# Spectrum, image and result moved in whole-partition transfers, the last product's rows in the spectrum's buffer, and a new order of steps

## The chip, the cores and the metric

The kernel runs on one core of one Trainium2 chip. The metric is the time of one execution on the device in microseconds (us). Its engines are TensorE (PE, matrix products; PEld is its weight load), VectorE (DVE), ScalarE (ACT), GpSimd (POOL) and SyncE (SP), which issues nearly all DMA transfers here.

## The reference

Input is x, 64 images of 96 channels and 56 x 56 pixels, f32. Three blocks follow one another, each on the whole image:

- A convolution block: a 1 x 1 product to 192 channels with a folded batch norm and silu; groups of channels shifted by one pixel and shuffled; a depthwise 3 x 3 convolution plus an identity branch, silu; a gate from the channels' means (two small grouped products, sigmoid); a 1 x 1 product back to 96 channels, plus x, silu.
- A spectral block over the 3136 pixels as one sequence: layer norm and a product to 192 channels with relu, a Fourier transform along the pixels, a complex diagonal product with biases and relu on each frequency, the inverse transform, a product back to 96 channels, added to its input.
- A feed-forward block with a layer norm in front, whose operands are rounded to 8-bit floats (5 exponent bits) and whose sums are rounded to 16 bits.

The Fourier transform of length 3136 is made as 56 x 56: a transform over one index (`f1`), twiddle factors and a transform over the other index (`f2`); only 29 of 56 rows of frequencies are kept, since the input is real. Between `f1` and `f2` the data must change from "rows on partitions" to "columns on partitions". That is done by storing to DRAM and loading back; the same is done on the way back, between `i1` and `i2`.

## The kernel before

One image is cut into steps, each a small function. `x_in` loads; `ea`, `eb` (first product), `eb_sh` (shift by DMA), `dw` (depthwise taps on PE), `gt` and `lt` (depthwise taps on DVE, 9 steps each), `se1`, `se2` (gate), `pj` (product back). Then `c`, `sp` (norm statistics), `w1`, `f1`, `f1_st` (store of the spectrum), `f2_ld` (its load), `f2`, `w2` (product), `i1`, `i1_st`, `i2_ld`, `i2`. Then `n`, `x`, `h`, `o` (norm, transposes, feed-forward) and `o_st`. A suffix tells the engine's part: `_mm` is PE, `_ev`, `_u`, `_r`, `_sq` are mostly ACT evacuations, `f2_s`, `f2_p`, `w1_ev`, `i2_ev`, `h_b`, `n_v`, `pj_add` are DVE.

The order of everything is written out by hand: `PLAN` gives each step of an image a time, image b adds b x 105, and all steps of all 64 images are issued in the order of these sums, under a manual schedule. Only the order counts; each engine then runs its list in order and waits where it must. Four images are in work at once, so `f2` of one image stands beside `dw` of the next one and `h` of the one before. `h_mm[6]` is the step h_mm with index 6.

Buffers that the steps share:

- `buf_h` holds, one after the other, `h_v` (output of `w1`), `pq_a` and `pq_b` (output of `f2_p`, read by `w2_mm`), and `p_v` (rows loaded by `i2_ld`, read by `i2_mm`).
- `buf_g` holds `g_v` (spectrum loaded by `f2_ld`, read by `f2_mm`), then `u_v` (output of `w2_ev`, read by `i1_mm`) and `q_v` (output of `i1_ev`, stored by `i1_st`).
- `psa`, two PSUM buffers in turn, takes the results of `w1`, `f1`, `f2`, `w2`, `i1` and `i2`; `psb`, four buffers, those of all other products.

The spectrum is loaded in four chunks of 8 (the last 5) frequency rows. Before each but the first, a tiny DMA that reads the chunk before (`probe`) keeps SP from issuing the next one until that one has landed. `f2_mm[0]` needs chunk 0, `f2_mm[2]` and `[1]` chunk 1, `f2_mm[3]` chunk 2, `f2_mm[4]` and `[5]` chunk 3:

```python
LD = ((0, 8), (8, 16), (16, 24), (24, NK))
def f2_ld(b, i):
    k0, k1 = LD[i]
    if i:
        nc.sync.dma_start(out=probe[0:1, 0:1], in_=g_v[64:65, LD[i - 1][0], 0:1])
    for r in range(2):
        nc.sync.dma_start(
            out=g_v[r * 64 : r * 64 + HW, k0:k1, :], in_=held["spec", b][:, r * 32 + k0 : r * 32 + k1, :]
        )
```

The 96 channels stand on partitions 0 to 47 and 64 to 111 of 112, so image and result are moved in two halves; partition 48 of the image holds ones inside the frame (it carries the first product's bias).

Of the kernel before, what the change touches and what calls it, by code (L numbers as in the profile page):

```python
# [7 lines left out]
F32 = mybir.dt.float32  # L8
# [7 lines left out]
C = 96  # L16
HW = 56
NPIX = HW * HW
MID = 192
HID = 384  # L20
CP = 112
TILES = ((0, 64), (64, CP))
GAP = 48
TP = 64
RPC = 8
NCH = HW // RPC
# [20 lines left out]
    "x_in": (-47.0873800, -43.2480721, -33.8184146, -42.4321669, -41.6983245, -49.6354125, -45.2970245),  # L47
    "ea_mm": (25.6687554, -18.6019459, -18.2766274, 16.8947317, 9.0890490, -20.9491366, 26.5234594),
    "ea_ev": (26.5961203, -12.8346944, -12.0558905, 18.3539585, 11.9892739, -18.0927155, 26.8208273),
    "eb_mm": (-24.2217280, -27.1252465, -28.5212136, -26.0439145),  # L50
    "eb_ev": (-24.1705572, -24.8159248, -27.0548028, -24.4210050),
    "eb_sh": (-7.7763780, -5.1891020, -14.3493101, -8.0736385),
    "eb_z": (-0.0568513,),
    "dw_mm": (27.1905859, 28.2270849, 30.0157383),
    "dw_ev": (32.6265507, 32.5419044, 34.0136867, 32.0626837),
    "gt": (
        18.5417590, 27.3932657, 28.4348554, 30.0405776, 30.3534777, 31.2679969, 32.1252342, 33.5617949, 35.3971287,
    ),
    "gs": (37.3295953,),
    "lt": (-3.4369246, 1.4154043, 8.9015990, 12.7386339, 14.9242937, 16.9569681, 19.0058087, 25.8181102, 27.2536815),  # L60
    "ls": (30.9696760,),
    "se1_mm": (38.1174920,),
    "se1_ev": (39.4012005,),
    "se2_mm": (39.9568261,),
    "se2_ev": (41.0093676,),
    "se2_th": (41.6370568,),
    "se2_pw": (42.7356286,),
    "pj_mm": (47.6293895, 48.0460084, 55.6924205, 56.2257124),
    "pj_add": (51.9548047, 52.9757229, 48.9486048, 52.4199992, 56.5208084, 56.3342891, 57.7357223, 58.9053497),
    "pj_ev": (52.4266468, 54.5563910, 49.5686264, 53.9975302, 57.3353294, 58.0358601, 64.2278724, 60.1034130),  # L70
    "c_mm": (68.6422640, 72.8958869, 66.4186663, 70.5016788, 73.7968378, 81.1540053, 75.3642593),
    "c_st": (69.1048996, 74.0834508, 69.6641726, 71.8469708, 79.6401411, 81.2770733, 76.3014887),
    "c_v": (77.3368996, 84.7421070),
    "c_pow": (80.4785931, 85.6468413),
    "sp_v": (83.0231830, 86.9442643),
    "sp_mm": (83.5958606, 91.6622997),
    "sp_ev": (84.6935666, 98.3470105),
    "sp_st": (84.9182307, 104.3262665),
    "w1_mm": (91.1847046, 99.3743923, 107.0630638, 109.7535225, 115.0779331, 117.7791802, 128.3897698),
    "w1_ev": (95.1158413, 101.3844416, 109.5428488, 112.4130173, 118.6707781, 121.0948441, 130.1859056),  # L80
    "f1_mm": (103.1645366, 103.6378920, 112.1950558, 112.9967147, 121.9973686, 123.2339179, 131.7418102),
    "f1_ev": (103.8752244, 106.2876092, 115.0341529, 116.5416927, 123.1240239, 126.3577447, 132.9203119),
    "f1_st": (105.0265754, 116.1773780, 117.6886644, 118.9203869, 126.8918215, 126.9985321, 135.1083565),
    "f2_ld": (135.1419010, 135.4933209, 140.1563600, 153.2148099),
    "f2_mm": (135.3144599, 144.2623043, 142.7071223, 149.0540458, 153.9987769, 158.4518856),
    "f2_u": (
        137.6614180, 139.5999755, 145.8963285, 148.6480681, 143.6745056, 144.3798314, 151.9081888, 154.2916813,
        154.8766840, 155.4088772, 160.1561499, 160.2407000,
    ),
    "f2_s": (  # L90
        140.6001249, 141.6781807, 148.1048425, 149.2120807, 145.7714192, 145.9139389, 152.5732992, 154.5515294,
        156.3172941, 156.6391862, 160.5955754, 160.7678822,
    ),
    "f2_r": (143.2110272, 151.0363931, 149.4970293, 156.5551535, 160.8170295, 165.3808270),
    "f2_p": (145.3432078, 151.4176571, 149.5496523, 158.2621001, 161.1258051, 167.6494558),
    "w2_mm": (159.7753575, 155.3022495, 161.7965796, 168.1185810),
    "w2_ev": (161.2536676, 157.1569605, 163.6822311, 171.1138835),
    "i1_mm": (162.6590790, 166.7961018, 174.2991711),
    "i1_ev": (166.3472470, 165.9292538, 169.1177355, 169.1485805, 176.9253459, 176.6408078),
    "i1_st": (174.9466660, 180.3925690, 182.4974982),  # L100
    "i2_ld": (188.6796396, 198.8294222),
    "i2_mm": (192.8792346, 192.2221249, 201.7637940, 200.8210782),
    "i2_ev": (197.2438881, 196.4091824, 193.4196408, 195.1684356, 205.0085736, 204.5692890, 201.3823970, 201.8192486),
    "n_mm": (199.2735303, 219.3462979, 198.1616011, 209.7155720, 217.1048197, 206.4557874, 216.1525940),
    "n_sq": (200.3838494, 223.0303187, 198.7625009, 212.4039709, 219.3987946, 208.1995030, 218.5954397),
    "n_v": (200.8599777, 223.0993290, 200.2251649, 217.3989652, 220.1840919, 209.9338724, 219.1855594),
    "n_pow": (201.5854245, 224.4817921, 203.3394463, 218.3771210, 221.4663650, 210.8600116, 220.4581247),
    "n_x": (204.8989415, 227.0802149, 207.1755708, 219.2080326, 226.6324331, 212.4013872, 223.1334093),
    "x_mm": (205.9313777, 228.0541936, 214.7407205, 222.1417630, 227.6089704, 214.9482177, 224.9828165),
    "x_ev": (215.5949267, 230.5744237, 217.0784037, 224.8320339, 228.9853364, 216.6319969, 227.3901209),  # L110
    "h_mm": (
        232.6842970, 233.0509672, 234.5689910, 233.8905234, 243.9705701, 231.1824963, 242.0876641, 249.3422780,
        247.6714562, 262.3158746, 249.5121590, 269.1269742, 245.6772976, 281.8579222, 275.5176718, 291.0115353,
        298.8948961, 298.6901683, 272.9130353, 274.8890827, 267.7027131,
    ),
    "h_ev": (
        233.2951821, 233.9892274, 235.1790311, 235.3740739, 245.7427623, 232.8851785, 246.7755713, 250.3102318,
        248.5727503, 264.8834302, 250.8738180, 272.1122460, 247.3449184, 285.4922975, 280.0758001, 292.5182940,
        298.9075518, 299.1057623, 275.2554216, 280.8510059, 271.9477751,
    ),  # L120
    "h_b": (
        233.3310183, 238.5879932, 239.6985884, 236.4106010, 248.1860080, 237.7565907, 247.4859421, 252.4799898,
        253.3286109, 265.1753247, 274.5160827, 273.6196081, 259.8167793, 289.1079857, 281.7059923, 295.2166748,
        313.0427147, 307.8153028, 280.3205727, 295.0172563, 303.2860349,
    ),
    "h_q": (
        235.1365714, 240.0903826, 240.2123523, 238.6786534, 249.8236945, 239.5739109, 249.1205248, 258.5058367,
        256.0111952, 266.4473323, 276.4671451, 279.2778238, 261.0771312, 290.1247931, 282.3662819, 298.7249474,
        314.1209334, 326.2464381, 296.9278791, 328.6751318, 314.9292593,
    ),  # L130
    "o_mm": (243.3019756, 251.4566128, 260.0349491, 292.9513206, 292.0855692, 335.3427890, 334.7225136),
    "o_ev": (252.4449030, 252.4462979, 260.7877533, 295.5347424, 297.3701267, 339.4824442, 335.9297802),
    "o_b": (253.4669270, 274.1077430, 267.6272919, 297.7581544, 311.6604822, 343.9355403, 344.9555045),
    "o_f": (256.7737436, 286.0913549, 285.2670749, 323.3039842, 337.3903643, 352.8603345, 353.4120892),
    "o_st": (258.9714075, 288.2940604, 307.3848207, 328.4555594, 347.7179313, 355.7939648, 378.3559833),
# [4 lines left out]
def conv_attn_ffn(  # L140
# [30 lines left out]
    tab_ones: bass.AP,  # L171
# [20 lines left out]
    nc.vector.memset(xi, 0.0)  # L192

    def load_x(b, i):

        rows = slice(i * RPC, (i + 1) * RPC)
        for p0, c0 in ((0, 0), (64, 48)):
            nc.sync.dma_start(  # L198
                out=xi[p0 : p0 + 48, 1 + i * RPC : 1 + (i + 1) * RPC, 1 : HW + 1],
                in_=x[b, c0 : c0 + 48, :].rearrange("c (a b) -> c a b", b=HW)[:, rows, :],  # L200
            )


    def load(ap, shape, name, eng=nc.sync, dtype=F32):
        t = const.tile(shape, dtype, name=name)
        eng.dma_start(out=t, in_=ap)
        return t

    ex_w = load(expand_t, [CP, MID], "ex_w")

    nc.sync.dma_start(out=xi[GAP : GAP + 1].rearrange("p a b -> p (a b)"), in_=tab_ones)
    for i in range(NCH):
        load_x(0, i)
    eps = const.tile([128, 1], F32, name="eps")
    nc.vector.memset(eps, 1e-5)
    mhalf = const.tile([128, NJ], F32, name="mhalf")
# [966 lines left out]
```

## Time and profile before

| | |
|---|---|
| median of 3 runs | 6605.18 us (6599.12 to 6605.9) |
| profiled execution, its own time | 6600.45 us |
| its span in the profile | 6598.6 us |
| mean granted TensorE clock | 0.973 |
| DMA packets | 976826, of them 641745 under 512 bytes; 740.73 MB |

Busy time of PE by step, from the groups by line between 2320 and 4317 us (20 images), divided by 20 and by the number of such steps in an image, in us: `ea_mm` 0.85, `eb_mm` 0.80, `dw_mm` 3.28 (three), `se1_mm` 0.54, `se2_mm` 0.78, `pj_mm` 1.8, 3.8, 2.1, 1.2, `c_mm` 0.50, `sp_mm` 0.26, `w1_mm` 1.52, `f1_mm` 0.81, `f2_mm` 2.03 (1.89, 1.65 and 1.27 for [1], [4] and [5]), `w2_mm` 2.4 (the last 1.6), `i1_mm` 1.75, `i2_mm` 1.28, `n_mm` 0.81, `x_mm` 0.34, `h_mm` 0.30, `o_mm` 0.69. They add up to 98.8 us an image, more than the PE busy time, because neighbouring lines overlap in the records. For DVE and ACT the mean of one instruction is taken: `lt` 1.86, `gt` 1.51, `w1_ev` 0.95, `f2_s` 1.30 and `f2_p` 1.10 (two instructions each), `i2_ev` 0.62, `n_v` 0.72, `h_b` 0.37, `pj_add` 0.57; `f2_u` 0.69, `f2_r` 0.9, `h_ev` 0.56, `h_q` 0.58, `pj_ev` 0.63, `w2_ev` 0.79, `o_b` 0.68, `dw_ev` 0.87, `gs` 1.44. These overlap by some 10%, too.

How to read the profile: the page's line of busy time gives an engine's busy time, its share of the span and its number of instructions. In the windows view a row is a stretch, its length, the busy time and number of instructions of PE, PEld, DVE, ACT and POOL, then the granted clock, the DMA engines' share and GB/s. In the waits view "A <- B: t, n, m" says that A's engine sat idle for B, t us in all, n times, m the longest. In the chain of waits each row is a start, a length and what ran; SPq is SP issuing. L numbers are lines of the kernel before.

### The profile page before, as it was taken

The page shows a single profiled execution, that of the slowest core. Times are in us where ns is not written, and L with a number is a line of the kernel's source. Part 1 is how long each engine was busy: PE and PEld are TensorE (multiplying, and loading weights), DVE is VectorE, ACT ScalarE, POOL GpSimd, SP SyncE. Part 2 cuts the span into 40 slices and gives each one's busy share as a digit, 9 for nine tenths or more (in the row PEclk, how much of TensorE's full clock was granted, in tenths as well). Part 3 has the DMA queues.
Part 4 walks back from the last instruction along what each step waited for, and adds up shares of the span by engine and source line. Part 5 has one row for each costly group of instructions (what it writes and reads, how often), then busy time and mean ns, then how long its engine had stood idle before and what let it go on. Part 6 is the DMA issues. An engine that isn't in the chain of part 4 may idle for free.

```text
span 6598.6 us, 217772 instructions
## 1 busy us (share of the span) xinstructions
PE 5970.6 (90%) x92162; PEld 4023.3 (61%) x92162; DVE 5271.5 (80%) x9939; ACT 4990.7 (76%) x10830; POOL 1660.2 (25%) x1100
## 2 busy tenths in 40 slices
PE   4999999999999999999999999999999999999986
PEld 2666666666666666666666666666666666666664
DVE  6788787787887887887877878878878878778773
ACT  2677777777777777777777777777777777777776
POOL 1122222222222222222222222222222222222222
PEclk8999999999999999999999999999999999999997
DMA  3444444444444444444444444444444444444442
GB/s 83 105 113 119 112 110 120 117 107 118 114 116 116 116 114 115 112 116 113 110 121 117 107 118 114 116 116 111 118 111 109 123 112 111 120 118 106 121 103 74
DMA packets 976826, 740.73 MB, mean 112 GB/s; under 512 B 641745, under 2 KB 916889, under 8 KB 975721
## 3 DMA queue, kind: packets, MB, share of 16 engines
q1 hardware_dynamic: 973130, 725.03, 44.4%
q8 instruction: 725, 11.88, 0.8%
q10 hardware_dynamic: 2720, 1.77, 0.1%
q14 instruction: 251, 2.06, 0.1%
HBM read 329.68 MB, written 341.31 MB: 102 GB/s over the span
## 4 chain that ended last, share of the span: by engine, by line
DVE 30%; DMA 21%; ACT 21%; PE 13%; SPq 6%; issue 6%; POOL 3%; DVEq 0%; POOLq 0%; ACTq 0%
DMA buf_g<-spec 10%; DVE d_last L508 7%; DMA buf_h<-rows 6%; DVE ue L799 4%; DVE s L796 4%; ACT y L954 4%; ACT ue L780 3%; PE ps_eb L421 3%; DMA spec<-fs 3%; POOL rs L922 3%; PE psa L755 3%; ACT h L965 2%; DVE buf_h L809 2%; SPq L198 2%; DVE buf_h L692 2%
## 5 line engine op out<-in xcount | busy, mean ns | idle before, releaser
L987 POOL TENSOR_TENSOR o<-t,o 112x448 f32<-112x448 f32 x448 | 684.2, 1528 | 3322.6 <-ACT o L981 2100.4
L508 DVE SCALAR_TENSOR_TENSOR d_last<-e_b,taps,d_last 128x1568 f32<-128x1568 f32 x512 | 954.3, 1864 | 0.5
L965 ACT CAST h<-y 128x448 fp8e5<-128x448 f16 x1344 | 756.2, 582 | 236.8 <-DVE y L959 224.5
L922 POOL TENSOR_TENSOR rs<-v,mhalf 128x4 f32<-128x4 f32 x448 | 609.8, 1374 | 926.4 <-DVE v L623 669.9
L954 ACT CAST y<-ps_h 128x448 f16<-128x448 f32 x1344 | 679.4, 556 | 161.2 <-PE ps_h L949 158.1
L495 DVE SCALAR_TENSOR_TENSOR d_vec<-e_a,taps,d_vec 128x1120 f32<-128x1120 f32 x512 | 770.8, 1505 | 11.6
L687 PE MATMUL psa<-w1c,t 112*128 112x192 f32 x3584 | 684.9, 334 | 9.9 <-DVE t L906 9.7
L755 PE MATMUL psa<-l_tab,buf_g 128*64 128x112 f32 x7424 | 477.1, 287 | 233.0 <-DMA buf_g<-spec 191.6
L755 PEld LDWEIGHTS psa<-l_tab,buf_g 128*64 128x64 f32 x7424 | 419.9, 153 | 409.4 <-issue 271.8
L474 PE MATMUL ps_d<-e_a,diag 32*32 32x504 f32 x18432 | 629.4, 590 | 0.0
L929 ACT ACTIVATE xt<-ps_n,rs 128x96 fp8e5<-128x96 f32 x1792 | 465.4, 377 | 198.6 <-POOL rs L922 190.1
L687 PEld LDWEIGHTS psa<-w1c,t 112*128 112x128 f32 x3584 | 579.8, 190 | 50.8 <-DVE t L906 17.5
L959 DVE TENSOR_SCALAR y<-y,qb 128x448 f16<-128x448 f16 x1344 | 472.1, 371 | 112.7 <-ACT y L954 103.5
L809 DVE SCALAR_TENSOR_TENSOR buf_h<-ue,s 128x448 f32<-128x448 f32 (+2 forms) x768 | 423.7, 600 | 159.6 <-ACT s L803 157.9
L637 DVE BATCH_NORM_STATS2 st<-ps_c 128x6 f32<-128x96 f32 x1792 | 326.2, 251 | 278.7 <-PE ps_c L629 272.4
L474 PEld LDWEIGHTS ps_d<-e_a,diag 32*32 32x32 f32 x18432 | 395.7, 103 | 214.9 <-ACT e_a L411 37.9
L780 ACT ACTIVATE ue<-psa,fa 128x448 f32<-128x448 f32 (+1 forms) x512 | 346.5, 690 | 229.6 <-PE psa L755 124.7
L692 DVE SCALAR_TENSOR_TENSOR buf_h<-psa,rs 128x768 f32<-128x768 f32 x448 | 426.8, 953 | 69.6 <-PE psa L687 69.6
L656 POOL TENSOR_TENSOR rs<-v,mhalf 128x16 f32<-128x16 f32 (+1 forms) x128 | 333.6, 2606 | 582.8 <-DVE v L651 582.8
L949 PE MATMUL ps_h<-xq,q 96*128 96x448 fp8e5 x1344 | 409.1, 360 | 72.3 <-ACT y L954 45.3
L796 DVE SCALAR_TENSOR_TENSOR s<-psa,fa,ue 128x448 f32<-128x448 f32 (+1 forms) x512 | 325.5, 636 | 181.3 <-ACT ue L780 180.8
L906 DVE SCALAR_TENSOR_TENSOR t<-psa,bn2c_b,t 112x392 f32<-112x392 f32 x512 | 291.7, 621 | 155.2 <-PE psa L894 151.9
(172 smaller groups left out, 11948.6 us busy)
## 6 DMA issues: line engine op xcount, KB each, us to landing
spec<-fs SPq DMA_DIRECT2D x896, 192.0 KB
buf_g<-spec SPq DMA_DIRECT2D x384, 336.0 KB
buf_h<-rows SPq DMA_DIRECT2D x128, 672.0 KB
x<-in_x SPq DMA_DIRECT2D x896, 84.0 KB
out_dram<-o SPq DMA_DIRECT2D x896, 84.0 KB
rows<-buf_g SPq DMA_DIRECT2D x128, 420.0 KB
rows<-buf_g SPq DMA_DIRECT2D x64, 504.0 KB
e_b<-e_u SPq DMA_DIRECT2D x256, 105.1 KB
```

The lines of the kernel that those rows point to most:

```text
L474: nc.tensor.matmul(pss[r][j * 32 : j * 32 + 32], lhsT=diag[pr, tap, :], rhs=e_a[pr, r0 : r0 + SR, dx : dx + HW], start=tap == 0, stop=tap ...
L495: nc.vector.scalar_tensor_tensor(d_vec, win, w, d_vec, ALU.mult, ALU.add)
L508: nc.vector.scalar_tensor_tensor(d_last, win, w, d_last, ALU.mult, ALU.add)
L687: nc.tensor.matmul(ps[:, k, 0:MID], lhsT=t[:, n0 : n0 + 2 * TP], rhs=w1c, start=True, stop=True)
L692: nc.vector.scalar_tensor_tensor(h_v[:, js, :], held.pop(("w1", b, g))[:, :, 0:MID], 0.0, held["v", b][1][:, js].unsqueeze(2).to_broadcast ...
L755: nc.tensor.matmul(ps[c0 : c0 + 64, k, 0:CP], lhsT=g_v[:, k1, c0 : c0 + 64], rhs=l_tab[:, k1, :], start=True, stop=True,)
L796: nc.vector.scalar_tensor_tensor(held["s", b, i][:, q, 0:n, :], im, par[:, m : m + 1], a, ALU.mult, ALU.add)
L809: nc.vector.scalar_tensor_tensor(pq[:, k0 : k0 + n, q * HW : q * HW + HW], ue[:, q, 0:n, :], 0.0, s[:, q, 0:n, :], ALU.max, op)
L922: nc.gpsimd.tensor_tensor(rs, held.pop(("nv", b, g)), mhalf[:, 0:4], ALU.pow)
L954: nc.scalar.copy(y16, held.pop(("h", b, i)))
L965: nc.scalar.copy(held["h8", b, j][:, m, :], held.pop(("y", b, i)), saturate=False)
L987: nc.gpsimd.tensor_tensor(o32, rows, o16, ALU.add)
```

## The change

- The spectrum's DRAM copy is laid out as 28 blocks of 128 rows. `f1_st` stores with one transfer from 128 partitions instead of two from 64, `f2_ld` loads a chunk with one transfer to 112 partitions instead of two to 56. The rows of the table for `f2` (`l`) are permuted to match.
- The image is handed over with its frame of zeros, its row of ones and its gap, as 112 rows of 58 x 58; it is loaded in 7 transfers of whole frame rows instead of 14. The memset of the image buffer and the table of ones are dropped. The result is stored as 112 rows in 7 transfers instead of 14, and the gap is cut away outside.
- `p_v` moves from `buf_h` to `buf_g`, over `u_v`.
- All times in `PLAN` are new. Some of them stand below.

```diff
 PERIOD = 105.0000000
 PLAN = {
-    "x_in": (-47.0873800, -43.2480721, -33.8184146, -42.4321669, -41.6983245, -49.6354125, -45.2970245),
+    "x_in": (-24.2443000, -22.8269900, -21.6203000, -18.5451800, -17.4513500, -26.3523900, -14.5291200),
...
-    "f1_mm": (103.1645366, 103.6378920, 112.1950558, 112.9967147, 121.9973686, 123.2339179, 131.7418102),
-    "f1_st": (105.0265754, 116.1773780, 117.6886644, 118.9203869, 126.8918215, 126.9985321, 135.1083565),
-    "f2_ld": (135.1419010, 135.4933209, 140.1563600, 153.2148099),
-    "f2_mm": (135.3144599, 144.2623043, 142.7071223, 149.0540458, 153.9987769, 158.4518856),
+    "f1_mm": (111.0795400, 114.9877200, 122.9002500, 131.7032800, 133.3588200, 144.9675200, 159.2674800),
+    "f1_st": (121.3074600, 123.5826000, 132.4558700, 132.4568700, 156.6125200, 156.9196400, 165.5183000),
+    "f2_ld": (165.5193000, 167.2513600, 168.4781000, 171.6838000),
+    "f2_mm": (165.5305000, 170.0123200, 167.4385600, 173.5398700, 175.0809900, 181.0757100),
...
-    "f2_r": (143.2110272, 151.0363931, 149.4970293, 156.5551535, 160.8170295, 165.3808270),
-    "w2_mm": (159.7753575, 155.3022495, 161.7965796, 168.1185810),
+    "f2_r": (168.1518300, 174.6694900, 171.0893300, 177.2582000, 179.9699800, 186.7982200),
+    "w2_mm": (178.6733900, 180.8602200, 186.8454400, 187.8914300),
...
-    "i1_mm": (162.6590790, 166.7961018, 174.2991711),
-    "i1_st": (174.9466660, 180.3925690, 182.4974982),
-    "i2_ld": (188.6796396, 198.8294222),
-    "i2_mm": (192.8792346, 192.2221249, 201.7637940, 200.8210782),
+    "i1_mm": (181.8710800, 188.8030600, 191.6809100),
+    "i1_st": (189.4814300, 193.5917400, 203.3721700),
+    "i2_ld": (203.3731700, 215.5533000),
+    "i2_mm": (210.4319200, 208.8235300, 216.3390900, 217.2505700),
...
-    nc.vector.memset(xi, 0.0)
...
-        rows = slice(i * RPC, (i + 1) * RPC)
-        for p0, c0 in ((0, 0), (64, 48)):
-            nc.sync.dma_start(
-                out=xi[p0 : p0 + 48, 1 + i * RPC : 1 + (i + 1) * RPC, 1 : HW + 1],
-                in_=x[b, c0 : c0 + 48, :].rearrange("c (a b) -> c a b", b=HW)[:, rows, :],
-            )
+        rows = slice(1 + i * RPC if i else 0, 1 + (i + 1) * RPC if i < NCH - 1 else PAD)
+        nc.sync.dma_start(out=xi[:, rows, :], in_=x[b, :, rows, :])
...
-    p_v = buf_h[:, 0 : NJ * C].rearrange("p (b o) -> p b o", o=C)
...
+    p_v = buf_g[:, 0 : NJ * C].rearrange("p (b o) -> p b o", o=C)
...
-            held["spec", b] = dram.tile([HW, 64, MID], F32, tag="spec", name="spec")
-        fs = held.pop(("fs", b, g)).rearrange("p j d c -> p (j d) c")
-        for e in range(2):
-            n0 = g * 8 + e * 4
-            nc.sync.dma_start(
-                out=held["spec", b][n0 : n0 + 4].rearrange("b k c -> k b c"), in_=fs[e * 64 : e * 64 + 64]
-            )
+            held["spec", b] = dram.tile([NJ, 128, MID], F32, tag="spec", name="spec")
+        nc.sync.dma_start(
+            out=held["spec", b][g * 4 : g * 4 + 4].rearrange("n p c -> p n c"),
+            in_=held.pop(("fs", b, g)).rearrange("p j d c -> p (j d) c"),
+        )
...
-        for r in range(2):
-            nc.sync.dma_start(
-                out=g_v[r * 64 : r * 64 + HW, k0:k1, :], in_=held["spec", b][:, r * 32 + k0 : r * 32 + k1, :]
-            )
+        rows = held["spec", b].rearrange("n (x k) c -> (n x) k c", k=32)
+        nc.sync.dma_start(out=g_v[0:CP, k0:k1, :], in_=rows[:, k0:k1, :])
...
-        for p0, c0 in ((0, 0), (64, 48)):
-            nc.sync.dma_start(
-                out=out[b, c0 : c0 + 48, j * CH : (j + 1) * CH],
-                in_=o32[p0 : p0 + 48].rearrange("p a b -> p (a b)"),
-            )
+        nc.sync.dma_start(out=out[b, :, j * CH : (j + 1) * CH], in_=o32.rearrange("p a b -> p (a b)"))
...
-    l[0:HW, :, 0:HW], l[0:HW, :, HW:] = co, -si
-    l[64 : 64 + HW, :, 0:HW], l[64 : 64 + HW, :, HW:] = si, co
+    at = n // 8 * 16 + n % 4 * 4 + n // 4 % 2 * 2
+    l[at, :, 0:HW], l[at, :, HW:] = co, -si
+    l[at + 1, :, 0:HW], l[at + 1, :, HW:] = si, co
```

## The prediction

> **What bounds the kernel now.** I read the page's first part, then the windows of the steady middle, the waits, the chain of waits, and the timeline of one image. The first two say that the tensor engine (PE) is nearly full:
>
> ```profile
> PE 5970.6 (90%) x92162; PEld 4023.3 (61%) x92162; DVE 5271.5 (80%) x9939; ACT 4990.7 (76%) x10830; POOL 1660.2 (25%) x1100
> ```
>
> ```profile
> 300.00:6300.00 6000.00, 5539.12 (x86084) 3737.34 (x86080) 4893.60 (x9191) 4647.65 (x10099) 1539.99 (x1018) 0.98 0.46 115
> ```
>
> Two landings of the same load stand one image apart in the chain below, 3318.59 and 3418.45: 99.86 us an image. PE is busy 5539.12 / 6000 of that, 92.2 us; 7.7 us are idle. 64 images take 6391 us; 209 us of the 6598.6 us span are fill and drain. The profiled execution took 6600.45 us, 0.07% under the median of 6605.18; all sums here start from 6600. A change below 0.2% (13 us, 0.2 us an image) can't be told from none.
>
> Which waits make up the 7.7 us? The waits view, PE rows (total, times, longest):
>
> ```profile
> PE psa L755 <- DMA buf_g<-spec: 191.6, 128, 9.8
> PE psa L894 <- DMA buf_h<-rows: 78.0, 61, 5.0
> PE ps_o L971 <- ACT t L599: 46.6, 57, 1.0
> PE psa L755 <- DVE ue L799: 31.5, 43, 1.8
> ```
>
> Divided by 64: 2.99 us an image for the spectrum's load, 1.22 for the load of the last product's rows; no other above 0.8. The chain of waits, in order of time (start, us, what), shows both:
>
> ```profile
> 3318.59 5.91 DMA buf_h<-rows
> ...
> 3354.18 0.57 SPq L730
> 3354.80 2.70 DMA spec<-fs
> 3357.94 5.35 DMA buf_g<-spec
> 3363.31 0.67 SPq L739
> 3364.46 5.30 DMA buf_g<-spec
> 3369.89 2.87 PE psa L755 x32
> ...
> 3418.45 6.42 DMA buf_h<-rows
> ```
>
> Two store issues, a landing, two load issues, a landing, the probe, the next two, a landing: chunk 1 is there 16.5 us after the last `f1_mm` ended (3353.29 to 3369.83). PE has 9.8 us of `dw_mm` and 3.9 more between those two points. VectorE (DVE) is close behind:
>
> ```profile
> 3328.90:3371.07 42.17, 38.03 (x591) 24.64 (x590) 40.36 (x45) 34.53 (x80) 13.75 (x9) 0.99 0.42 108
> ```
>
> From the first products of an image to `f2_s[1]` DVE works 40.36 of 42.17 us. So a DMA that lands earlier only helps if DVE's list up to there is shorter too. The numbers below for stretches of the order are my sums: steps standing between two points in PLAN's order, times the step table above.
>
> **Spectrum's store and load: 2.5 us an image off.** One store issue instead of two: 0.61 us. A chunk's load goes from issue to issue in 6.46 us (3357.56 to 3364.02). The trace has 112 packets of 6144 bytes in it, 405 ns each, and 28 of 4 bytes, 14 a half; a store pair has 32, 16 a half. I read this as 14 DMA engines for 56 rows, 16 for 64: 112 rows in one transfer would need 45.4 / 16 = 2.84 us instead of 3.24. At least that 0.4 us comes off, at most also the second issue (0.44) and its long stay of 1.36: 1.8. I take 1.3, because the packets really ran from 3358.50 to 3362.64, 4.1 us, which is the serial two halves. Chunk 1 then lands 16.5 - 0.6 - 2 x 1.3 = 13.3 us after `f1_mm[6]`. The new order has less PE work ahead of it: `dw_mm` 9.84, `f2_mm[0]` 2.03, three `h_mm` 0.90, together 12.8 (13.8 before), plus 0.4 to 1.1 of waiting for `dw_ev` as now. Chunk 2 is due at 18.5, PE comes at 18.6. I leave 0.5 of the 2.99. Bounds: 1.0 (if a load gains only 0.4, chunk 1 lands at 15.1) to 3.0.
>
> For DVE: from the second half's `i2_ev` to `f2_s[1]` the old order has 47.3 us of instructions, the new one 44.1 (one `lt`, one `w1_ev` and one `h_b` now stand ahead). That is room for the 2.5.
>
> **The product's rows in buf_g: 1.0 off.** Nothing new is moved; `i2_ld` now waits for `i1_mm`'s reads of `u_v`, which are over before `i1_st` is issued, and `f2_ld` for the last `i2_mm`, some 50 us earlier in the order. buf_h is free after `w2_mm`, so `w1_ev` no longer waits for `i2_mm`. The waits on rows: before, 10.5 us of PE work stand between `i1_mm[2]` and the first `i2_mm`, and 6.6 to the second load's; after, 13.2 and 8.9. The longer of the two waits in the images I looked at was 1.76 us, the second load's, less than the 2.3 gained. I take 1.0; bounds 0 (i2_ld[1] stands behind `eb_sh` and `sp_st` on SP, as before) and 1.22.
>
> **The clock: 0.6 off.** After the wait for chunk 1, `f2_mm[2]` needs 2.85 us for 32 matmuls, `f2_mm[0]` 1.75. The windows of both, the granted clock third from the end:
>
> ```profile
> 3363.40:3365.20 1.80, 1.77 (x33) 1.66 (x34) 1.76 (x2) 1.76 (x6) 0.00 (x0) 1.00 0.26 34
> 3369.80:3372.80 3.00, 2.91 (x35) 2.66 (x36) 2.96 (x6) 1.81 (x5) 1.30 (x1) 0.59 0.37 73
> ```
>
> The clock's record has half speed for 215 of those 6000 us, 63 spells of 3.41 us, about one an image, here after waits of 1.85 and 1.76 us. Without those waits I expect half the spells to go: 0.6 (0 to 1.1). The Trainium skill, "TensorE: Matmul & The Clock Gate", Part 1, has the clock halved only after an idle window of about 3.4 us; no gap in this image is that long, so by it nothing would be won here and the forecast would be 6440. The rows go against it.
>
> **The f2 stretch: 1.0 on.** From `f2_mm[1]` to `w2_mm[3]` the old order keeps 30.4 us of PE steps beside the chain `f2_u`, `f2_s`, `f2_r`, `f2_p`; the new one 25.7 (five `h_mm`, an `o_mm`, an `i1_mm` and `se2_mm` fewer). DVE has 26.1 there (27.4), ACT 26.1 (31.3). The chain took 31.1 us, from 3371.07 to 3402.20, of which DVE idled 2.46:
>
> ```profile
> 3401.39 0.81 DVE L809 SCALAR_TENSOR_TENSOR buf_h<-ue,s 128x280 f32<-128x280 f32 x2 [2.46 <-ACT s L803]
> ```
>
> `f2_r[5]` stood behind three `pj_ev` there; in the new order it stands ahead of all four. 31.1 - 2.46 - 1.3 = 27.3. PE's 30.4 ran in 30.0 with 1.5 of waits, so 25.7 need 24.1: 3.2 of waits, 1.7 more than now. Part of the chain's length was PE's own; I take 1.0, bounds 0 and 5.5.
>
> **Costed at nothing.** Images in 7 transfers: the 5376 pieces of 224 bytes an image took 96.5 us of packet time, 784 longer ones at the 94 ns of a 1792-byte piece take 74; the engines are 46% busy. The Trainium skill, "DMA: Bandwidth & Descriptors", Specifications, says that pieces under 512 bytes cost a read-modify-write; here they take 18 ns against 32 for 512 bytes, so little was lost, and off the path. The loads now come later: x_in[2] needs `pj_add[4]` and `[6]`, about 3.5 us of DVE after `pj_mm[3]`, an issue of 0.45 and 2.55 to land (6.5), and `ea_mm[1]` comes after 10.6 of PE work; x_in[4] is due at 9.7, `ea_mm[4]` comes at 12.3. Without that cover each us is 64. Behind a waiting x_in on SP stand `i1_st` and `i2_ld`, as before. SP has 25 issues fewer an image. The memset and the row of ones are gone once, under 4 us. The order is 13 us deeper from first matmul to last store: 0 to 13 us, in the range.
>
> **Sum.** 2.5 + 1.0 + 0.6 - 1.0 = 3.1 us an image, 198 us: 6600 - 198 = 6402, say 6400.
>
> **Rivals.** (1) Slower: the f2 chain sets the pace. For it: PE's filler shrinks by 4.7 us exactly where ACT and DVE hand over six times, each group waiting for the one two before it in the two `psa` buffers. Against: ACT's list is 5.2 us shorter there. If the chain stays at 31.1 us, PE waits 7.0 instead of 1.5: 5.5 lost against 4.1 won, +90 us, 6690. It decides from 29.7 us of chain. (2) Hidden: DVE does not get to `f2_s[1]` earlier. It was there at 3371.07 and PE started `f2_mm[1]` at 3373.25, so part of term one becomes a wait for DVE; 0.5 us an image remain, 6570. Also the case that a one-piece load is no quicker. (3) More: no loss in the f2 stretch, all of 2.99, 1.22 and 1.1 won: 5.3, 6260.
>
> **Numbers.** Chances: forecast (6320 to 6500) 0.52, (1) 0.26, (2) 0.13, (3) 0.09. Range 6260 to 6690: nearly all of the forecast, all of (2), half of (1) and of (3), 0.8. Faster by over 0.2%: 0.52 + 0.09 + 0.05 of (2) + 0.01 = 0.67; within: 0.05; slower 0.28.
>
> **What would show it.** Right: the wait of `f2_mm` on the load under 1 us an image, that of `i2_mm` under 0.4, chunk to chunk about 5.2 us, 16 four-byte packets a load, half-speed spells halved, PE idle about 4.5 us. Wrong: PE waits on `ue`, `t` or `buf_h` in the f2 stretch above 3 us (rival 1), or at `f2_mm[1]` (rival 2); waits on the image loads; an image above 99.9 us.

## The result, and the profile after

The change made the kernel slower: 6701.17 us (median of 4 runs, 6692.36 to 6702.09) against 6605.21 us for the kernel before on the same chip, a ratio of 1.0144 (95% interval 1.0127 to 1.0162). The forecast was 6400 us, the range 6260 to 6690. The profiled execution has a span of 6699.4 us.

All figures "an image" below are means over images 8 to 55 of a trace; differences in us between kernels are differences of their ratios to the kernel before, times 6605. A ratio is known to about 0.15%, so such a difference to some 14 us.

The page's line of busy time, and the windows row of the same 6000 us as before:

```profile
PE 6086.0 (91%) x92162; PEld 4078.4 (61%) x92162; DVE 5387.1 (80%) x9938; ACT 5013.4 (75%) x10830; POOL 1852.7 (28%) x1100
```

```profile
300.00:6300.00 6000.00, 5552.33 (x84646) 3727.98 (x84640) 4922.52 (x9048) 4594.56 (x9943) 1699.07 (x1001) 0.97 0.43 118
```

An image takes 102.04 us instead of 100.44. PE is busy 94.48 of it (92.70 before) and idle 7.56 (7.74): the idle time that was to be won is still there, and the same work takes 1.8 us more. The waits of PE, the rows that matter (total, times, longest):

```profile
PE ps_x L924 <- ACT xt L917: 85.4, 65, 1.7
PE ps_h L937 <- ACT d L475: 72.2, 107, 1.0
PE psa L743 <- DMA buf_g<-spec: 58.0, 53, 8.8
PE psa L679 <- ACT fs L711: 45.7, 61, 1.1
...
PE ps_se L526 <- ACT red L517: 38.2, 64, 0.7
...
PE psa L882 <- DMA buf_g<-rows: 26.1, 33, 3.4
```

The two waits that the change was read against did fall: the spectrum's load from 191.6 to 58.0 us, the rows from 78.0 to 26.1. Above and around them stand short waits for ACT; `x_mm` for `xt`, 20.7 us before, is now the longest of all. It is the wait of one step, `x_mm[1]`: 1.35 us an image, none before. The new `PLAN` sets `n_pow[1]` (GpSimd), `n_x[1]` (ACT) and `x_mm[1]` (PE) directly one behind the other, so little covers that chain, and `n_pow[1]` takes 2.45 us there instead of 1.0 (GpSimd beside VectorE, below, tells why):

```profile
3407.61 2.45 POOL L910 TENSOR_TENSOR rs<-v,mhalf 128x4 f32<-128x4 f32 x1 [2.30 <-DVE v L615]
3411.17 0.36 PE L924 MATMUL ps_x<-eye,xt 128*96 128x112 fp8e5 x4 [1.34 <-ACT xt L917]
```

The timeline of PE in one image, from the end of `dw_mm` to the projection (start, length, what; in brackets the idle time ahead of it and what ended it):

```profile
3428.47 1.75 PE L743 MATMUL psa<-l_tab,buf_g 128*64 128x112 f32 x32
...
3430.86 0.35 PE L937 MATMUL ps_h<-xq,q 96*128 96x448 fp8e5 x1 [0.31 <-ACT d L475]
3432.13 0.35 PE L937 MATMUL ps_h<-xq,q 96*128 96x448 fp8e5 x1 [0.93 <-ACT d L475]
3432.70 2.75 PE L743 MATMUL psa<-l_tab,buf_g 128*64 128x112 f32 x32 [0.22 <-DMA buf_g<-spec]
3435.39 0.55 PE L937 MATMUL ps_h<-xq,q 96*128 96x448 fp8e5 x1
3435.97 0.64 PE L510 MATMUL ps_se<-sums,rd_w 128*24 128x1 f32 x12
3437.13 0.71 PE L526 MATMUL ps_se<-red,ep_w 24*32 24x1 f32 x40 [0.52 <-ACT red L517]
...
3438.56 3.26 PE L753 MATMUL psa<-l_tab,buf_g 128*64 128x112 f32 x32
3441.61 2.64 PE L743 MATMUL psa<-l_tab,buf_g 128*64 128x112 f32 x32
```

Two stretches of that, with the granted clock third from the end:

```profile
3436.00:3438.60 2.60, 2.08 (x59) 1.58 (x59) 1.19 (x4) 2.60 (x6) 0.00 (x0) 0.50 0.79 243
3438.60:3441.80 3.20, 3.20 (x36) 3.20 (x37) 3.16 (x7) 2.07 (x5) 0.00 (x0) 0.50 0.32 81
```

Chunk 1 keeps `f2_mm[2]` waiting for only 0.22 us. But `h_mm[6]`, `se1_mm`, `se2_mm` and `h_mm[10]` now stand between it and `f2_mm[1]`, which then runs at half clock: 3.26 us for 32 matmuls that take 1.75 in `f2_mm[0]`.

### The profile page after: what moved, and what is told of

Read it like the earlier page. It is cut to its first block, busy times and chain, and to the rows that moved or that the text cites. A ratio compares the mean times of both kernels' runs of the same rounds, so it can differ in the third digit from the quotient of the medians.

```text
span 6699.4 us, 216194 instructions
## 1 busy us (share of the span) xinstructions
PE 6086.0 (91%) x92162; PEld 4078.4 (61%) x92162; DVE 5387.1 (80%) x9938; ACT 5013.4 (75%) x10830; POOL 1852.7 (28%) x1100
## 4 chain that ended last, share of the span: by engine, by line
DVE 37%; PE 32%; ACT 13%; DMA 8%; POOL 4%; issue 4%; SPq 2%; POOLq 0%; DVEq 0%; ACTq 0%
DVE d_last L500 8%; DVE d_vec L487 7%; PE psa L847 5%; POOL rs L910 4%; PE psa L808 4%; DVE s L784 3%; DVE ue L787 3%; DVE buf_h L684 3%; DVE v L614 3%; ACT ue L768 3%; DMA buf_g<-spec 3%; PE ps_ea L398 3%; PE psa L743 3%; PE ps_eb L413 2%; DVE buf_h L797 2%
## 5 line engine op out<-in xcount | busy, mean ns | idle before, releaser
L975 POOL TENSOR_TENSOR o<-t,o 112x448 f32<-112x448 f32 x448 | 768.8, 1716 | 2711.4 <-ACT o L969 2295.1
L500 DVE SCALAR_TENSOR_TENSOR d_last<-e_b,taps,d_last 128x1568 f32<-128x1568 f32 x512 | 996.4, 1946 | 0.4
L910 POOL TENSOR_TENSOR rs<-v,mhalf 128x4 f32<-128x4 f32 x448 | 723.5, 1677 | 844.8 <-DVE v L615 831.4
L947 DVE TENSOR_SCALAR y<-y,qb 128x448 f16<-128x448 f16 x1344 | 428.8, 327 | 159.0 <-ACT y L942 158.6
L466 PEld LDWEIGHTS ps_d<-e_a,diag 32*32 32x32 f32 x18432 | 419.1, 103 | 205.3 <-ACT o L964 48.5
L937 PE MATMUL ps_h<-xq,q 96*128 96x448 fp8e5 x1344 | 428.2, 369 | 98.7 <-ACT d L475 72.2
L711 ACT COPY fs<-psa 128x768 f32<-128x768 f32 x448 | 367.1, 819 | 72.6 <-PE psa L699 57.7
L699 PE MATMUL psa<-buf_h,f_tab 56*64 56x384 f32 x3584 | 395.6, 512 | 17.6 <-DVE buf_h L684 17.6
```

Of the source, the lines that this page charges most:

```text
L466: nc.tensor.matmul(pss[r][j * 32 : j * 32 + 32], lhsT=diag[pr, tap, :], rhs=e_a[pr, r0 : r0 + SR, dx : dx + HW], start=tap == 0, stop=tap ...
L500: nc.vector.scalar_tensor_tensor(d_last, win, w, d_last, ALU.mult, ALU.add)
L910: nc.gpsimd.tensor_tensor(rs, held.pop(("nv", b, g)), mhalf[:, 0:4], ALU.pow)
L975: nc.gpsimd.tensor_tensor(o32, rows, o16, ALU.add)
```

## The experiments

E1 is the old order with all the rest of the change; "spec" is the kernel before with the spectrum's transfers alone.

**Which part costs?** Four kernels take the change apart. In the old order:

```diff
 # e1_old_order: the changed kernel
-PLAN = {...new times...}
+PLAN = {...times of the kernel before...}
 # e4_spec: the kernel before; e7_spec_rows adds the last pair
-    two f1_st / f2_ld transfers of 64 / 56 partitions, old l
+    one of 128 / 112 partitions, permuted l
-    p_v = buf_h[:, 0 : NJ * C]
+    p_v = buf_g[:, 0 : NJ * C]
```

> The changed kernel with the old list of times (PLAN) put back: new transfers, padded image and result, rows in buf_g, old order. Theory (the loss lies in the new order of the instructions, the transfers and the buffer gain what the waits show): the two waits still fall, f2_mm on the spectrum load by about 2.1 us an image and i2_mm on the rows by 0.8, and nothing is given back in x_mm, h_mm and w1_mm; 6605 - 64 x 2.9 = 6420 us, 6400 to 6500. Rival A (the new transfers or the shared buffer cost as much as they gain, or slow the clock): 6650 to 6720, as the changed kernel. Rival B (the transfers were hidden by other work and the times are needed to use them): within 20 us of 6605.

> The kernel before with the spectrum stored and loaded in transfers over all partitions (and the table's rows to fit), nothing else changed: old order, rows in buf_h, image and result unpadded. Theory: the wait of f2_mm on the spectrum load falls from 2.99 us an image to 0.5 to 1.5, and the time by most of that: 6605 - 64 x 2 = 6480 us, 6440 to 6540. Rival A (the transfers cost): 6605 to 6700. Rival B (another wait takes its place within the old order): 6580 to 6610.

> The kernel before with the spectrum's transfers over all partitions and the last product's rows in buf_g: old order, image and result unpadded. Against the run with the spectrum alone this is the buffer's share. Theory: the first row load no longer waits for the last readers of buf_h but for i1's reads of u in buf_g, i2_mm's wait on the rows falls by 0.8 us an image: 50 us below the run with the spectrum alone, so 6430. Rival A (a load into buf_g waits for i1_st's reads or for other work there): 0 to 60 us slower than with the spectrum alone. Rival B: no difference over 10 us.

And the new order without the rest (`PLAN` of the changed kernel, and `p_v` in `buf_g`, in the kernel before):

> The kernel before with the new list of times alone; the last product's rows lie in buf_g too, as the new times start the following image's w1_ev earlier. The spectrum goes by the old two transfers of 56 partitions, image and result unpadded. Theory (the order loses): slower than the changed kernel by what the spectrum's transfers are worth in its order, 6701 + 64 x 2 = 6830 us, at least 6750. Rival A (the transfers lose, the order is neutral or gains): 6605 or less. Rival B (the order was made for late data, and nothing of the transfers matters): 6700.

| kernel | median, us | ratio to before (95%) |
|---|---|---|
| spectrum's transfers, old order (e4) | 6510.77 | 0.9843 (0.9826 to 0.9860) |
| and rows in `buf_g` (e7) | 6530.99 | 0.9878 (0.9858 to 0.9897) |
| and image, result padded (e1) | 6534.63 | 0.9876 (0.9858 to 0.9895) |
| and the new order: the change | 6701.17 | 1.0144 (1.0127 to 1.0162) |
| new order, rows, old transfers (e3) | 6872.46 | 1.0386 (1.0367 to 1.0405) |

So the spectrum's transfers win 104 us, the buffer loses 23, padding is nil, and the new order loses 177. In the new order the transfers, with the padding, are worth 160 us. That settles the main question: the loss lies in the order, not in the data's new paths. e4 came out within its range; e7, expected 50 us under e4, is 23 over it, as its rival A had it; e3 is slower still than its 6830. e1 was expected at 6420; it missed by the size of two terms, both to be seen in its waits:

```profile
PE psa L882 <- DMA buf_g<-rows: 126.0, 69, 5.0
PE psa L743 <- DVE ue L787: 62.9, 64, 1.8
...
PE psa L743 <- DMA buf_g<-spec: 36.7, 40, 8.3
PE psa L753 <- DVE ue L787: 32.6, 33, 1.3
```

The load's wait is nearly gone, but `f2_mm` now waits 95.5 us for VectorE's `f2_s` (`ue`) instead of 33.6, so a part of the win comes back there. And the wait for the rows is longer than before (126.0 against 78.0 us; 89.9 in the kernel with the spectrum alone). What goes with its fall in the changed kernel is the new order, which puts more products between `i1_mm[2]` and `i2_mm[1]` (PE busy 13.05 us there, 10.95 in e1), not the buffer. Why rows in `buf_g` cost 0.3 us of wait an image in the same order stays open.

Where the order loses it, stretch by stretch (us an image, from start to start; a figure shifts by up to 0.1 with the images that are taken):

| from, to | before | spec | e1 | after |
|---|---|---|---|---|
| end of `f1_mm[6]`, `f2_mm[2]` | 17.07 | 14.95 | 14.93 | 14.54 |
| `f2_mm[2]`, `f2_mm[1]` | 3.09 | 3.09 | 3.21 | 5.44 |
| `f2_mm[1]`, `w2_mm[3]` | 30.26 | 31.08 | 30.83 | 26.77 |
| `w2_mm[3]`, next `i2_mm[1]` | 14.15 | 14.09 | 13.96 | 17.55 |
| `i2_mm[1]`, `w1_mm[0]` | 2.84 | 2.84 | 2.84 | 5.15 |
| `w1_mm[0]`, end of `f1_mm[6]` | 33.03 | 33.11 | 34.00 | 32.59 |
| an image | 100.44 | 99.16 | 99.77 | 102.04 |

The 2.5 us that the load wins in the first row of the changed kernel are gone in the second: `f2_mm[1]` starts 19.98 us after `f1_mm[6]`, as before (20.16), while in e1 it starts at 18.14. The 3.5 won in the third row return in the fourth, as products that were taken out there stand here.

**The squeeze products ahead of `f2_mm[1]`.** Times of `PLAN` in the changed kernel:

```diff
-    "se2_mm": (62.7563500,)
+    "se2_mm": (65.0133200,)      # behind f2_mm[1]
-    h_mm[10] 272.9590900
+    h_mm[10] 272.6400000         # ahead of se1_mm
```

> The changed kernel with three instructions moved in its order: h_mm[10] ahead of the first squeeze product (se1_mm), and the second one (se2_mm) behind f2_mm[1] instead of ahead of it, as the old order has it. Theory (about half of what the order loses is half clock, 5.3 us of half speed an image in the f2 products against 2.4 in the old order, and the idle time at se1 and se2 keeps the clock low): half speed falls to 2 to 3.5 us an image, 6701 - 64 x 1.2 = 6625 us, 6590 to 6660. Rival A (the clock follows the load wait ahead of f2_mm[0] and f2_mm[2] alone): half speed stays at 5, and the time within 20 us of 6701. Rival B (se2's result comes later and the projection waits for it): 6700 to 6740.

Measured 6744.65 us, ratio 1.0198 (1.0183 to 1.0213): 36 us slower than the change. `f2_mm[1]` did start earlier (19.14 us), and half speed fell from 5.2 to 4.5 us an image, but `se1_mm` now stood 4.1 us behind `f2_mm[2]` instead of 3.2, and `pj_mm[0]` came 6.0 us after `f2_mm[1]` instead of 4.9. That is rival B: the projection waits longer, so the gate's chain, and not the f2 products alone, has a part in setting that stretch. The run made both moves at once and doesn't part them.

**GpSimd beside VectorE.** `o_f` adds one row of eight only:

```diff
-        o32 = work.tile([CP, RPC, HW], F32, tag="o32", name="o32")
-        rows = by_columns(b).rearrange("p b a -> p a b")[:, j * RPC : (j + 1) * RPC, :]
-        nc.gpsimd.tensor_tensor(o32, rows, o16, ALU.add)
+        o32 = o_two[b * NCH + j & 1]      # two buffers, set to zero once
+        rows = by_columns(b).rearrange("p b a -> p a b")[:, j * RPC : j * RPC + 1, :]
+        nc.gpsimd.tensor_tensor(o32[:, 0:1, :], rows, o16[:, 0:1, :], ALU.add)
```

> The changed kernel with GpSimd's last addition (o_f) done on one row of eight; the other seven rows of the result are left at zero. Transfers and all other work are unchanged. Theory (in the new order GpSimd's o_f lies beside VectorE's gt, lt and sp_v, both slow down, and VectorE is on the path there): gt's slow instances (2.3 us against 1.37), lt's (2.7 against 1.84) and sp_v's 1.1 us fall back, VectorE's busy time falls by 2.5 us an image, the time by 40 to 110 us to 6590 to 6660. Rival (VectorE's longer time lies beside other work): under 20 us.

> The same light o_f (one row of eight, the rest left at zero) in the old order, with the changed kernel's transfers and buffer (6535 us with the whole o_f). Theory (in the old order o_f lies where it slows little that is on the path): VectorE's busy time falls by under 1 us an image, the time by 0 to 30 us, 6505 to 6535. Rival (GpSimd's part costs the same in both orders, so it explains nothing of their difference): the same fall as in the new order.

New order 6630.53 us (1.0029; 1.0018 to 1.0041), 76 us less; old order 6501.92 (0.9829; 0.9812 to 0.9845), 31 less. So some 45 us of the order's 177 go with GpSimd's additions. VectorE's busy time fell by 4.5 us an image in the new order and by 1.7 in the old one, in both more than expected. GpSimd's own list got shorter too (28.8 to 21.9 us an image in the new order, 25.7 to 23.1 in the old one), and these two runs don't part the two effects. How the one acts on VectorE is in the trace: `sp_v` (DVE, L653) in the changed kernel and, second line, in e1:

```profile
L653 DVE TENSOR_TENSOR dev<-v,rs x128: 160/1154/1271, 111.1 to 6546.8; 128x16 f32<-128x16 f32 x64, 128x12 f32<-128x12 f32 x64
```

```profile
L653 DVE TENSOR_TENSOR dev<-v,rs x128: 154/170/177, 105.4 to 6377.4; 128x16 f32<-128x16 f32 x64, 128x12 f32<-128x12 f32 x64
```

(min/median/max in ns.) The timeline of the changed kernel shows what runs beside it:

```profile
3478.17 1.30 POOL L975 TENSOR_TENSOR o<-t,o 112x448 f32<-112x448 f32 x1
```

```profile
3478.23 1.27 DVE L653 TENSOR_TENSOR dev<-v,rs 128x16 f32<-128x16 f32 x1 [0.79 <-POOL rs L648]
```

An elementwise product of 16 columns lasts until `o_f` is over. `gt[7]` (2.31 us beside `o_f[6]`, 1.37 alone) and `lt[7]` (2.72 against 1.84) are two more. The Trainium skill, "SBUF — State Buffer", Who interferes with whom, says it so: a VectorE instruction with two SBUF inputs and a GpSimd one that reads SBUF block each other for a whole instruction, and the first to be issued wins. The rows agree, also the other way round: beside an `lt` that keeps its 1.84 us, `n_pow[5]` in the old order and `n_pow[1]` and `[3]` in the new one take 2.45 us instead of 1.0.

One addition alone, moved from behind `c_pow[1]` to behind `n_pow[0]`:

```diff
-    o_f[4] 320.9333100
+    o_f[4] 322.4900000
```

> The changed kernel with o_f[4] moved behind n_pow[0] on GpSimd, so that the second sp_v (1.13 us beside o_f[4], 0.16 alone) runs alone; nothing else changed. Theory (the stretch from i2_mm[1] to w1_mm[0], 0.6 us shorter an image with the light o_f, is shorter for that reason): 6701 - 64 x 0.4 to 0.7 = 6655 to 6675. Rival A (o_f[4] only takes the time from n_pow[3] or lt[0] later on): 6690 to 6730.

6667.23 us (1.0105; 1.0089 to 1.0122), 26 us less: `i2_mm[1]` to `w1_mm[0]` falls from 5.15 to 4.53 us as expected, and 0.28 of it comes back before `f1_mm[6]`.

**The half clock.** Idle products ahead of `f2_mm[2]`'s own, in its PSUM tile:

```diff
+        for k in range(5 if i == 2 else 0):      # 3 in the fill3 kernels
+            nc.tensor.matmul(ps[0:64, k, 0:CP], lhsT=eye[:, 0:64], rhs=l_tab[:, k, :], start=True, stop=True)
```

> The changed kernel with five idle products (112 columns each, about 0.26 us) ahead of f2_mm[2]'s own, into the same PSUM tile before its own products overwrite it; they wait for no transfer, so TensorE works where it would wait for the second part of the spectrum. Theory (the idle time of 1.8 us between f2_mm[0] and f2_mm[2] sets off the half clock that costs f2_mm[1] and f2_mm[3] 3.6 us an image, 11.02 + 9.72 us against about 8.5 each): half speed falls from 5.3 us an image to under 2.5, and the time by 60 to 110 us, to 6590 to 6640. Rival A (the idle time there is not what sets it off): half speed stays, and the products that the wait doesn't cover add 0 to 0.5 us an image, 6700 to 6735. Rival B (the half-speed stretch lies beside VectorE's work, which then ends last): half speed falls, and the time by less than 30 us.

> The same five idle products in the kernel before with the spectrum's transfers over all partitions (6511 us; half speed 1.6 us an image). Theory: half speed falls to under 0.5 us an image and the time by 20 to 50 us, 6460 to 6490. Rival A: 6500 to 6550. Rival B: half speed falls, time within 15 us of 6511.

> The changed kernel with both: the five idle products and the light o_f (one row of eight, the rest of the result left at zero). Theory (half clock and the shared time of VectorE and GpSimd are two separate costs of the new order): the sum of both falls, 6701 - 71 - 85 = 6545 us, 6510 to 6580; against the light o_f in the old order (6502) under 60 us of the order's 167 would stay unexplained. Rival (they are one cost, or neither is what the order loses): 6600 to 6640.

Each of the five is two instructions, and the ten take 1.17 us together; behind them `f2_mm[2]` still waits 0.62 us for the load in this image, and then runs at full speed:

```profile
3399.72 1.17 PE L740 MATMUL psa<-l_tab,eye 128*64 128x112 f32 x10
3401.51 1.75 PE L745 MATMUL psa<-l_tab,buf_g 128*64 128x112 f32 x32 [0.62 <-DMA buf_g<-spec]
```

Half speed fell from 303.8 us of 6000 to 116.0 in the changed kernel, and the time by 42 us to 6661.56 (1.0080; 1.0065 to 1.0096), less than the 60 expected at least. In the kernel with the spectrum alone half speed fell from 102.4 to 81.9 us and nothing changed (6512.85; 0.9854). With both the filler and the light `o_f` the time is 6594.5 (0.9977; 0.9967 to 0.9987), 110 us less, nearly the sum of the two (42 and 76). With three, where the expectations take a product as 0.52 us, which adds up durations that overlap (the three take 0.79 us together):

> The changed kernel with three idle products (1.56 us by the 0.52 us that each took in the run with five) ahead of f2_mm[2]'s own, under the 1.8 us that TensorE waits there. Theory (five were 0.8 us too long, so their 40 us understate what the half clock costs): half speed stays under 2.5 us an image and the time falls by 60 to 100 us, 6600 to 6640. Rival (f2_s on VectorE ends last behind f2_mm[1] and f2_mm[3], and the half clock lies mostly beside it): 6650 to 6675, as with five.

> The kernel before with the spectrum's transfers over all partitions and h_mm[17], h_mm[16] ahead of i2_mm[1] (6507 us), with three idle products ahead of f2_mm[2]'s own. Theory: half speed falls from 2.4 us an image to about 1, and with 1.0 us less filler than the run with five the time by 10 to 40 us, 6465 to 6495. Rival: 6500 to 6520, the f2 stretch follows VectorE.

> The changed kernel with both, three idle products and o_f[4] moved. Theory (two separate costs): the sum of the two falls, 6570 to 6610. Rival: no more than the better of the two alone, 6610 to 6660.

Three are too few to hold the clock up (204.8 us at half speed) and win 18 us: 6680.79 (1.0116; 1.0099 to 1.0133). With `o_f[4]` moved as well it is 6666.61 (1.0102; 1.0084 to 1.0120), no better than that move alone. In the old order the three win nothing (6502.76, 0.9850, against 0.9840 without them), as the rival had it, although half speed fell from 146.8 to 99.0 us. So the half clock costs at least some 20 to 40 us of the 177: going by the filler with five, nearly 190 us fewer at half speed bring 42, the filler's own time included. By pace it would be more: 32 matmuls take 3.26 us instead of 1.75, so nearly half of such time is lost, and the changed kernel has 157 us more of it than e1 (303.8 against 146.8), which makes an estimate of 70 us. Part of that lies beside the waits of the gate and of VectorE; how much, no run shows.

**The products that moved.** The stretch from `f2_mm[0]` to `pj_mm[0]` takes 14.9 us in the changed kernel and 15.0 in e1, with one `h_mm` and two `o_mm` less in it, 1.7 us by the table of steps. PE is busy for 11.7 us of it in both all the same, since more of it runs at half clock. Two runs move `o_mm[0]` and `o_mm[1]`: into it in the new order, out of it in the old one.

```diff
 # m1_cover_back: the changed kernel, o16 in four buffers
-    o_mm[0], o_mm[1] 282.4637100, 305.0722500
+    o_mm[0], o_mm[1] 271.0000000, 275.1000000
 # m2_cover_out: e1, h8 in four buffers
-    o_mm[0], o_mm[1] 243.3019756, 251.4566128
+    o_mm[0], o_mm[1] 267.7200000, 273.0000000
```

(`o_ev`, `o_b`, `o_f` and `o_st` follow where they must.)

> The changed kernel with o_mm[0] moved behind f2_mm[0] and o_mm[1] behind f2_mm[1], their o_ev after them, and four buffers for o16: 1.4 us of products an image from the stretches behind pj_mm[1] back into the one from f2_mm[0] to pj_mm[0]. Theory (this stretch follows the spectrum's loads and VectorE, and TensorE has room there): it stays within 0.5 us of its 14.9, the time falls by 64 x 0.7 to 1.2, 6620 to 6660 us, and half speed falls too. Rival (TensorE's work is the same wherever it lies, so the place of two products changes nothing): 6680 to 6720.

> The old order with the changed kernel's data (6535 us), with o_mm[0] and o_mm[1] moved out of that stretch to behind i1_mm[0] and i1_mm[1], where TensorE never idles; four buffers for h8. Theory: the stretch from f2_mm[0] to pj_mm[0] gets shorter by less than 0.6 us of its 15.0, the one from pj_mm[2] to c_mm[0] longer by 1.4, time up by 64 x 0.8 to 1.4, 6585 to 6625 us. Rival: 6520 to 6550.

Both are far slower, and outside all expectations: 6922.67 us (1.0472; 1.0458 to 1.0487) and 6817.09 (1.0319; 1.0304 to 1.0334). In m1 the wait of `h_mm` for a PSUM buffer, 24.9 us in the change, is the longest of all:

```profile
PE ps_h L937 <- ACT y L942: 168.1, 64, 2.8
```

The four `psb` buffers are taken in the order of the products: with `o_mm[0]` among them `h_mm[12]` meets a buffer that `h_ev` has not emptied, and waits 2.7 us an image instead of 0.9 (then for `dw_ev`). `f2_mm[0]` to `pj_mm[0]` grows to 19.0 us, half speed to 8.9 us an image. In m2 that stretch stays at 15.3 us although 1.4 us of products left it, which is what the theory said of it; but the products' new place, `pj_mm[2]` to `c_mm[0]`, grows by 3.6 us, 1.8 of them idle where PE never idled. Here too steps wait for PSUM buffers, `o_mm[1]`, `h_mm[11]` and `c_mm[0]` together 1.7 us an image more than in e1, and `f2_mm[2]` 0.9 more for the load. PE's busy time in the f2 stretch fell by 0.3 us only, as half speed grew from 2.4 to 5.6 us an image, and its idle time rose by 0.6. That fits a stretch whose length PE's work does not set; with so much else changed it is no clean proof. That the products moved out of it are what the order pays for is not shown, as neither place took them at their own price.

**A better version.** Two tries on the kernel with the spectrum alone:

> The kernel before with the spectrum's transfers over all partitions (6511 us) and h_mm[17] and h_mm[16] moved ahead of i2_mm[1], so that 0.6 us more of other products lies between the last i1 product and the wait on the rows. Theory (the rows' round trip ends last there, 1.28 us an image): the wait falls by 0.5 us an image, 6511 - 64 x 0.5 = 6480 us, 6465 to 6500. Rival (the two products only change places with the wait, which returns in i2_mm[2] and i2_mm[3] for the second half of the rows): 6500 to 6520.

> The kernel before with the spectrum's transfers over all partitions, and o_f[5] moved on GpSimd from beside gt[1] (2.42 us there against 1.38 without it) to after o_f[1], where VectorE idles; its store follows i2_ld[0], and o16 has four buffers. Theory (VectorE has no gap of over 1.4 us from w1_ev[1] to f2_s[1] and sets the pace there, so 1.0 us a image comes off): 6511 - 64 x 0.5 to 1.0 = 6445 to 6480 us. Rival (f2_mm waits for the spectrum's transfer anyway, which is not earlier): 6500 to 6515.

`h_mm[17]` and `[16]` ahead of `i2_mm[1]` (times 297.10 and 297.15): 6506.76 us (0.9840; 0.9827 to 0.9853), the same as without. The rival had the time right, not the reason: the wait for the rows did fall, from 89.9 to 36.3 us, but PE's busy time rose by 0.6 us an image and half speed from 102.4 to 146.8 us. `o_f[5]` late (391.2; its row block then adds a later image's t): 6719.58 (1.0167; 1.0152 to 1.0183). `gt[1]` did get faster (1.37 us), but `c_pow[0]` now stands behind `o_f[5]` on GpSimd and started 2.9 us after `c_v[0]` ended instead of 0.1: PE's `sp_mm` waited for VectorE's result instead.

```profile
PE ps_dev L666 <- DVE dev L647: 168.1, 63, 4.3
```

The best of all kernels are the spectrum's transfers in the old order, with or without the small moves (6511, 6507 and, with three idle products on top of c1, 6503 us; the ratios 0.9843, 0.9840 and 0.9850 are the same within their intervals), 1.5% under the kernel before and 3% under the change.

## Why the prediction was wrong

The forecast was 3.1 us an image off; measured is 1.6 on. The two loads' waits fell by 2.9 (forecast 3.5), new waits took 2.7 (forecast 1.0, in the f2 chain), and PE's busy time rose by 1.8 (forecast 0.6 off, the clock). So the loads were read nearly right, and what failed is the price of the new order. (The 99.86 us an image are one image's; the mean is 100.44, so fill and drain are some 170 us and not 209. The sum doesn't use that.)

**Spectrum, 2.5 forecast.** The mechanism was right, the size of the win not. The wait fell by 2.1 us an image, in e4 by 2.5 (191.6 to 30.8 us); alone, in the old order, the change is worth 104 us, 1.6 an image, within the bounds of 1.0 to 3.0. Chunk to chunk takes 5.7 us, not 5.2 (6.34 to 6.52 before): the serial halves did not cost the 1.3 that I took, 0.7 was there. The 16 four-byte packets a load are there. What caps it in e4 is VectorE: `f2_s[1]` ends 17.82 us after `f1_mm[6]`, as before (17.89), and `f2_mm[1]` starts 0.2 later; the waits of `f2_mm` for `ue` rose from 33.6 to 112.9 us, 1.2 an image. That is rival 2's mechanism, in part.

**Rows, 1.0 forecast.** The wait fell by 0.8, but the step gave the credit to the buffer. e7 shows the buffer alone at 23 us lost; the fall goes with products that the new order took from elsewhere.

**Clock, 0.6 off forecast.** Wrong in sign: 303.8 us at half speed instead of 215. (The 63 spells of the prediction are windows of 3.41 us; they make 54 spells, 9 of them of two windows.) I had tied the spells to the wait for chunk 1. The gaps ahead of them are smaller and several: in the image above 0.93 for a PSUM buffer, 0.22 for the load, 0.52 for `red`. The Trainium skill, "TensorE: Matmul & The Clock Gate", Part 1, has the clock halved after an idle window of about 3.4 us; in the 3.4 us ahead of the 57 spells of the change PE was idle for 1.57 us in the median, and the longest single gap was 0.93 us in the median and 2.02 at most. The measurement decides: much less will do. It is no sharp limit: windows that kept the clock had up to 1.73 us of idle time.

**f2 stretch, 1.0 on forecast.** This is the step that failed. I looked at `f2_mm[1]` to `w2_mm[3]`, and there I was right: the chain from `f2_s[1]` to `f2_p[5]` fell from 31.46 to 29.01 us and the stretch by 3.5. I did not price the two places on either side. From `f2_mm[2]` to `f2_mm[1]` the new order holds four other steps, and 2.35 us of what the load wins are spent there. And all other waits of PE were taken as they were: idle time fell by 2.9 us on the two loads and by 0.18 in all, so 2.7 us of waits are new, on ACT, on `se1`, `se2`, `x_mm`, `w1_mm`. The forecast had 1.0 for them, all in the f2 chain. The largest, `x_mm[1]`'s 1.35 us, lies far from it.

**Not in the sum at all.** PE's busy time rose by 1.78 us an image; by step, with the records of a line joined: `f2_mm` 0.53, `f1_mm` 0.47, `h_mm` 0.28, `ea_mm` 0.22. (Neighbouring lines overlap in the records, so these are no exact shares.) In `f2_mm` it goes with the half clock. In `f1_mm` it goes with the order: the first four instructions of a step take 533 ns, the others 482, except where another `f1_mm` stands ahead; the old order has two such pairs, the new one none. Step by step that is only 0.12 us an image; the rest of the 0.47 is that the two steps of a pair overlap in the records. And GpSimd's list was counted as off the path: 28.8 us an image instead of 25.7, and VectorE's 83.8 instead of 81.9.

**Rivals.** Rival 1 was to win if the f2 chain stayed above 29.7 us; it did not, and the kernel is slower all the same. Its place was nearly right, its mechanism not. At "costed at nothing", image and result cost 0 (e7 against e1) as forecast.

**What stays open.** Of the order's 177 us, some 45 go with GpSimd's additions and at least 20 to 40 with the half clock. With both taken away the new order is still at 0.9977, the old one with the light `o_f` at 0.9829: 98 us, in which the filler's own 1.2 us an image have a part that was not measured. The clock is not in it: half speed is 75.1 us there, 151.8 in the old order. The table of stretches says between which steps the 98 us lie, but no run isolates them. The nearest suspect is the wait of `x_mm[1]`, 1.35 us an image in that run too: 86 us if all of it were lost (an estimate, 64 x 1.35). No run moved that step.

## What to carry to other kernels

When a change comes with a new hand-written order, split it first: take the data paths in the old order and the new order on the old paths, and price each alone; here one half wins 1.6% and the other loses 2.7%. In a forecast, moved work is not free because its sum is the same: for each step count what now stands between it and the step that needs its result, on every in-order engine and in every rotation of buffers. A wait that disappears from one line is won only if the next anchor (here `f2_mm[1]`) starts earlier.

## What the runs showed that was not expected

- The TensorE clock halves for 3.41 us or a multiple of it after stretches of 3.4 us in which PE was idle for about half of the time (57 spells in 6000 us, 303.8 us; median 1.57 us idle, the longest gap 0.93 in the median).
- An elementwise product of 16 columns on VectorE takes 1.15 us instead of 0.17 beside a GpSimd addition that it has nothing to do with.
- In an order this tight, two products in another place cost 217 us (m1) and 293 us (m2). In m1 the wait of `h_mm` for a PSUM buffer that `h_ev` empties grew by 143 us; in m2 such waits are a part of it.
